# A message-passing layer on one NeuronCore: column addresses kept in DRAM, one resident copy of x, 72 and 68 gathered columns per step, register loads of eight

## The chip, the core and the metric

The kernel runs on one NeuronCore of a Trainium2 chip. The metric is the device time of one execution in microseconds (us). The kernel before takes 5184.74 us, the median of three runs (5167.56 to 5185.11). The profile is of a further execution, of 5200.1 us.

Five engines work side by side: TensorE (PE in the profile, PEld for its weight loads), VectorE (DVE), ScalarE (ACT), GpSimd (POOL) and SyncE (SP), which here only starts DMAs.

## The reference

There are 12500 nodes with 64 features, and 400000 edges sorted by their destination. Each edge has a source `src`, a destination `dst` and 16 features of its own.

```python
src, dst = (edge_index[0], edge_index[1])
m_in = jnp.concatenate([x[src], x[dst], edge_attr], axis=-1)
h = jax.nn.silu(m_in @ W1 + b1)
messages = jax.nn.silu(h @ W2 + b2)
agg = jax.ops.segment_sum(messages, dst, num_segments=x.shape[0])
node_in = jnp.concatenate([x, agg], axis=-1)
return jax.nn.silu(node_in @ W3 + b3)
```

The result is the layer normalisation of x plus what this returns. All of it is float32. The one irregular access is `x[src]`: 400000 rows of 64 numbers at random places.

## The kernel before, in words

**Steps.** The edges are cut into 3125 tiles of 128 edges, and eight tiles make an "oct". There are 391 octs. The main loop, `for o in range(NO + 1)`, issues one oct's work per turn, in a software pipeline. The order of instructions on TensorE, ScalarE, VectorE and SyncE is the order written in the loop. GpSimd's gathers run as far ahead as five buffers (`gat`) allow.

**Three ways to fetch x[src].** The product with the first part of W1 is made once for all nodes and kept in DRAM (`pa`, made by `table` during the first octs). From oct 12 (`RAW`) on:

- *Gathers.* GpSimd starts one indirect DMA for each tile (L373), which fetches 128 rows of `pa` into the buffer `ga`. TensorE later adds them to the oct's first product with an identity matrix (L454), which also frees the buffer.
- *Columns.* x is also held transposed in SBUF (`xs`). For some pairs of tiles, VectorE and ScalarE copy the columns of the 256 edges one by one into a tile `cx`: an instruction copies 64 partitions by 4 bytes, from an address that stands in a register. VectorE does it with a reduction over one element (L297), ScalarE with a copy (L299). TensorE multiplies `cx` by W1 (L451), and GpSimd leaves out these two tiles.
- *Rows.* SyncE starts 16 DMAs of one row per oct (L324); this makes one more pair of tiles in every 16 octs.

**How the columns are dealt.** In each oct VectorE makes 32 columns ahead of the copy `xw` (L402) and the comparison `eh` (L430), and 32 after them. ScalarE makes 32 ahead of the activation `h` (L458) and 28 ahead of the activation `m` (L473). That is 124 in an oct, so a pair of tiles is ready about every 2.06 octs. Ahead of the columns stands a load of registers on the same engine (L290), which reads edge addresses from SBUF. The first load of a run of columns takes 16 registers, the others 8:

```python
ACOLS = (32, 28)
VCOLS = (32, 32)
LOADS = (16, 8)
n = min(hi - lo, P - e0 % P, LOADS[lo > hi - todo])
```

**Where the addresses come from.** For each pair of tiles SyncE loads the 256 sources from DRAM (`index`), and two octs before their use VectorE turns them into byte addresses with two instructions (`address`, L359). The first tile of a pair has its columns read from partitions 0 to 63 of `xs`, the second from partitions 64 to 127, where a second copy of x stands. The second copy is loaded in octs 5 to 8 (`resident(1, c)`).

**VectorE's other work in an oct**: `agg` (L487, adds an oct's sums), `oh` (L424, a comparison ahead of the first columns), `xw` and `eh`. TensorE's first product of the next oct (L441) needs `oh` and `xw`.

Of the kernel before, what the change touches and what calls it, by code (L numbers as in the profile page):

```python
# [11 lines left out]
I32 = mybir.dt.int32  # L12
U8 = mybir.dt.uint8
AF = mybir.ActivationFunctionType
OP = mybir.AluOpType
# [5 lines left out]
P = 128  # L21
# [6 lines left out]
AHEAD = 3  # L28
RAW = 12
TABLES = 7  # L30
ACOLS = (32, 28)
VCOLS = (32, 32)
ROWS = 16
LOADS = (16, 8)
XBASE = (0, 64 << 18)
XADDR = 36864
LAG = CT * P // 32

U = 125
# [4 lines left out]
@with_exitstack  # L44
def kernel(
    ctx: ExitStack,
    tc: tile.TileContext,
    x: bass.AP,
    xt: bass.AP,
    src_c: bass.AP,  # L50
    src_row: bass.AP,
    dst_c: bass.AP,
    dst_row: bass.AP,
    attr_t: bass.AP,
    dst_2: bass.AP,
    attr_2: bass.AP,
    base: bass.AP,
    w1: bass.AP,
    b1: bass.AP,
    w2: bass.AP,  # L60
    b2: bass.AP,
    w3: bass.AP,
    b3: bass.AP,
    out: bass.AP,
    edges: int,
):

    nc = tc.nc
    N, D = x.shape  # L80

    const = ctx.enter_context(tc.tile_pool(name="const", bufs=1))
    dram = ctx.enter_context(tc.tile_pool(name="dram", bufs=1, space=DRAM))
    pa = dram.tile([N, D], F32, name="pa")
    badi = const.tile([1, 1], I32, name="badi")
    ident = const.tile([P, P], F32, name="ident")
    make_identity(nc, ident)

    with ExitStack() as inner:
        windows(inner, tc, ident, badi, pa, x, xt, src_c, src_row, dst_c, dst_row, attr_t, dst_2, attr_2, base, w1, b1, w2, b2, w3, b3, out, edges)  # L90

    flag = nc.values_load(badi[0:1, 0:1], min_val=0, max_val=2 * P,
                          skip_runtime_bounds_check_because="a count of partitions")
    with tc.If(flag > 0):
        general(tc, ident, x, xt, src_c, dst_c, dst_row, attr_t, w1, b1, w2, b2, w3, b3, out, edges)


def windows(ctx, tc, ident, badi, pa, x, xt, src_c, src_row, dst_c, dst_row, attr_t, dst_2, attr_2, base, w1, b1, w2, b2, w3, b3, out, edges):
    nc = tc.nc
    N, D = x.shape  # L100
    NP = xt.shape[1]
    A = attr_t.shape[0]
    TILES = edges // P
# [32 lines left out]
    for s in range(2):  # L136
        h = slice(s * D, (s + 1) * D)
        nc.scalar.dma_start(w1d[h, h], w1[0:D, :])
        nc.scalar.dma_start(b1s[h, :], b1.rearrange("(k o) -> k o", o=1))
    XC = 2048  # L140
    xs = fast.tile([P, NP], F32, name="xs")

    def resident(s, c):
        w = min(XC, NP - c)
        nc.scalar.dma_start(xs[s * D:(s + 1) * D, c:c + w], xt[:, c:c + w])

    resident(0, 0)
    for s in range(2):
        h = slice(s * D, (s + 1) * D)
        nc.scalar.dma_start(w2d[h, h], w2)  # L150
    resident(0, XC)
    w3x = const.tile([D, D], F32, name="w3x")
    b3r = const.tile([1, G, D], F32, name="b3r")

# [1 line left out]
    for s in range(3):  # L156
        part = const.tile([1, D], BF16, name=f"part{s}")
# [32 lines left out]


    agg = fast.tile([P, NP], F32, name="agg")

    bf = fast.tile([1, NO], F32, name="bf")
    nc.vector.tensor_copy(bf, bi)
# [40 lines left out]
    for k in range(3):  # L236
        t = fast.tile([P, P], F32, name=f"xw{k}")
# [10 lines left out]
    with tc.tile_pool(name="gat", bufs=AHEAD + 2) as gat, tc.tile_pool(name="drp", bufs=2) as drp, \  # L248
# [14 lines left out]
        while True:  # L263
            o = RAW + -(-2 * P * (len(pairs) + 1) // RATE) + 1
# [3 lines left out]
        cols, indices = {}, {}  # L268
        xb = xs.bitcast(U8)

        def columns(o, eng, part):
            if o < RAW:
                return
            lo = (o - RAW) * RATE
            if eng == ENG.Activation:
                lo, n = lo + sum(ACOLS[:part]), ACOLS[part]
            else:
                lo, n = lo + sum(ACOLS) + sum(VCOLS[:part]), VCOLS[part]
            hi, todo = lo + n, n
            while lo < hi:  # L280
                j, e0 = lo // (2 * P), lo % (2 * P)
                if j >= len(pairs):
                    return
                n = min(hi - lo, P - e0 % P, LOADS[lo > hi - todo])
                if pairs[j] not in cols:
                    cols[pairs[j]] = cx.tile([P, P], F32, name="cx")
                t = cols[pairs[j]].bitcast(U8)
                s = e0 // P
                h = slice(s * D, (s + 1) * D)
                _, regs = nc.values_load_multi_w_load_instructions(  # L290
                    indices[j][0:1, e0:e0 + n], engines=(eng,), min_val=XBASE[s] + XADDR,
                    max_val=XBASE[s] + XADDR + 4 * (N - 1), skip_runtime_bounds_check_because="src names a node")
                for e, r in zip(range(e0 % P, e0 % P + n), regs):
                    to, frm = t[h, 4 * e:4 * e + 4], xb[h, ds(r - (XBASE[s] + XADDR), 4)]
                    if eng == ENG.DVE:

                        nc.vector.tensor_reduce(to, frm[:, :, None], AX.X, OP.max)  # L297
                    else:
                        nc.scalar.copy(to, frm)  # L299
                lo += n  # L300


        rpairs = []
# [38 lines left out]
        def begun(o):  # L342

            first, behind = -(-(o - RAW) * RATE // (2 * P)), -(-(o + 1 - RAW) * RATE // (2 * P))
            return range(max(0, first), max(0, min(behind, len(pairs))))

        def index(o):
            for j in begun(o):
                t = cxi.tile([1, 2 * P], I32, name="cxi")
                e = octs[pairs[j]][1] * P  # L350
                nc.sync.dma_start(t, src_row[:, e:e + 2 * P])
                indices[j] = t

        def address(o):
            for j in begun(o):
                t = indices[j]
                for s in range(2):
                    h = slice(s * P, (s + 1) * P)
                    nc.vector.tensor_scalar(t[:, h], t[:, h], 4.0, float(XBASE[s] + XADDR), op0=OP.mult, op1=OP.add)  # L359

        winrow, winreg = {}, {}
        sums = psa.tile([P, 4, S], F32, name="pg")
# [71 lines left out]
        def first_layer(o):  # L434
            c, t0, n, first, last = octs[o]
            n2 = n + n % 2
            k = n2 // 2
            ga = got.pop(o)
            oh, eh = hots.pop(o)
            p1 = ps1.tile([P, OT // 2, P], F32, name="p1")  # L440
            nc.tensor.matmul(p1[:, :k], xw[o % 3], oh, start=True, stop=False, skip_group_check=True)  # L441
            if o < RAW:
                pt = mis.tile([P, OT // 2, P], F32, name="mm")
                for i in range(k):
                    nc.tensor.matmul(pt[:, i, :], ga[:, 2 * i:2 * i + 2, :].rearrange("p s d -> p (s d)"), ident,  # L445
                                     start=True, stop=True)
                xg = work.tile([P, OT // 2, P], F32, name="m")
                nc.vector.tensor_copy(xg[:, :k], pt[:, :k])
                nc.tensor.matmul(p1[:, :k], w1d, xg[:, :k], start=False, stop=True, skip_group_check=True)
            if o in pairs:  # L450
                nc.tensor.matmul(p1[:, 0, :], w1d, cols.pop(o), start=False, stop=False, skip_group_check=True)  # L451
            for i in range(1 if o in pairs else 0, k if o >= RAW else 0):
                g2 = single.pop(o) if o in rpairs and i == 1 else ga[:, 2 * i:2 * i + 2, :]
                nc.tensor.matmul(p1[:, i, :], g2.rearrange("p s d -> p (s d)"), ident,  # L454
                                 start=False, stop=(i == k - 1), skip_group_check=True)
            columns(o, ENG.Activation, 0)
            h = work.tile([P, OT // 2, P], F32, name="h")
            nc.scalar.activation(h[:, :k], p1[:, :k], AF.Silu, bias=b1s)  # L458
            made[o] = h, eh
# [138 lines left out]
        with tc.manual_schedule(engines={ENG.PE, ENG.Activation, ENG.DVE, ENG.SP}):  # L598
            compare_dst(0)
            compare_nodes(0)  # L600
            for o in range(NO + 1):
                if o == 0:
                    sources(0, slice(CT, SCT))
                    nc.sync.dma_start(dc[:, CT:SCT], dst_c[:, CT:SCT])
                for k in parts[3 * o - 3:3 * o] if o else []:
                    n = min(XC, NP - k)
                    nc.scalar.activation(agg[:, k:k + n], zero.to_broadcast([P, n]), AF.Copy)
                if o < 2:
                    for c in parts[2:5] if o == 0 else parts[5:]:
                        resident(0, c)  # L610
                if o == 3:
                    for s in range(2):
                        nc.scalar.dma_start(w3s[s * D:(s + 1) * D, :], w3[D:2 * D, :])
# [4 lines left out]
                if o == RAW:  # L618
                    nc.vector.memset(mv, 1.0)
                    nc.vector.memset(eps, 1e-5)  # L620
                if 5 <= o < 5 + (len(parts) + 1) // 2:
                    for c in parts[(o - 5) * 2:(o - 4) * 2]:
                        resident(1, c)
                index(o + 3)
                rload(o + 3)
                if o % (SCT // OT) == 6 and (o // (SCT // OT) + 1) * SCT < TILES:
# [15 lines left out]
                columns(o, ENG.DVE, 0)  # L642
                if o < NO:
                    first_layer(o)
                if o == 0:
                    nc.vector.tensor_copy(b2r, b2p[:, None, :].to_broadcast([3, OT, D]))
                if o + 1 < NO:
# [16 lines left out]
                    add_up(o - 2)  # L664
                if o >= 1:
                    second_layer(o - 1)
                address(o + 2)
                raddress(o + 2)
                rows(o)
                if o < NO:  # L670
# [294 lines left out]
```

## Time and profile before

| What | Value |
|---|---|
| median of three runs | 5184.74 us |
| profiled execution | 5200.1 us, span 5197.9 us |
| TensorE busy (matmul) | 2932.5 us, 56% |
| ScalarE busy | 2906.1 us, 56% |
| VectorE busy | 2641.3 us, 51% |
| GpSimd busy | 2565.3 us, 49% |
| mean granted TensorE clock | 0.629 |
| columns by VectorE (L297) | 24032, 150 ns each |
| columns by ScalarE (L299) | 22560, 188 ns each |
| gathers by GpSimd (L373) | 2619 from `pa`, 944 ns each |

"Busy" counts the time in which an engine executes an instruction. Loads of registers and the starting of DMAs are not counted as busy: they stand in the trace as work of the engine's queue (DVEq, ACTq). An idle time that ended without a semaphore that the profile sees is put down to "issue". The durations of neighbouring columns overlap, so their number times their mean is more than the busy time.

### The profile page before, as it was taken

How to read it: one execution, taken by the hardware profiler on the slowest of the kernel's cores; microseconds unless marked ns; L12 is line 12 of the kernel's file. 1: busy time of each engine (PE TensorE's matmuls, PEld its weight loads, DVE VectorE, ACT ScalarE, POOL GpSimd, SP SyncE). 2: the span in 40 equal slices, each digit the busy share in tenths (PEclk: the TensorE clock that was granted, in tenths of full speed). 3: DMA queues.
4: the chain of work that ended last, by engine and by line, in shares of the span. 5: the costliest groups of instructions: out<-in, count | busy, mean ns of one | idle time of the engine just before them, and what ended most of it. 6: DMA issues, size and time to landing. Idle time of an engine off the chain costs nothing. (4 is left out here: it accounts for less than half of the span.)

```text
span 5197.9 us, 107486 instructions
## 1 busy us (share of the span) xinstructions
PE 2932.5 (56%) x15131; PEld 2075.4 (40%) x15131; DVE 2641.3 (51%) x26395; ACT 2906.1 (56%) x23402; POOL 2565.3 (49%) x2724
## 2 busy tenths in 40 slices
PE   5655655555555555555564655656555555555566
PEld 3443434434433344343343434434433343344344
DVE  1255555545555555555555555555555555555555
ACT  1255555555555655655556565555556555655555
POOL 5544454454444544445444444545454444555453
PEclk7666565666666666666656566565656666665656
DMA  4321111211211121122112211211211221121121
GB/s 85 86 46 39 40 39 40 47 39 40 46 42 43 40 46 40 40 43 42 41 40 49 43 40 42 44 39 40 47 40 40 44 47 40 40 47 39 40 46 40
DMA packets 203943, 229.98 MB, mean 44 GB/s; under 512 B 133612, under 2 KB 141988, under 8 KB 202324
## 3 DMA queue, kind: packets, MB, share of 16 engines
q1 hardware_dynamic: 101528, 122.61, 10.5%
q0 software_dynamic: 86880, 89.14, 9.1%
q10 hardware_dynamic: 14812, 11.26, 0.9%
q14 instruction: 595, 4.87, 0.3%
q8 instruction: 128, 2.10, 0.2%
HBM read 216.36 MB, written 6.40 MB: 43 GB/s over the span
## 5 line engine op out<-in xcount | busy, mean ns | idle before, releaser
L373 POOL DMA_INDIRECT ga<-pa,sc x2619 | 2472.2, 944 | 2516.1 <-PE p L454 1699.8
L299 ACT COPY cx<-xs 64x4 uint8 x22560 | 2404.2, 188 | 1406.1 <-issue 1362.4
L297 DVE TENSOR_REDUCE cx<-xs 64x4 uint8 x24032 | 1910.3, 150 | 1806.6 <-issue 1740.9
L441 PE MATMUL p<-oh,xw 128*128 128x512 f32 (+1 forms) x782 | 772.4, 1089 | 1529.3 <-DVE xw L402 727.6
L441 PEld LDWEIGHTS p<-oh,xw 128*128 128x128 f32 x782 | 187.1, 297 | 1637.1 <-DVE xw L402 776.3
L482 PE MATMUL pg<-eh,m 128*64 128x48 f32 x6250 | 363.0, 277 | 588.6 <-ACT m L473 174.1
L454 PEld LDWEIGHTS p<-ident,ga 128*128 128x128 f32 x2620 | 591.3, 314 | 194.9 <-issue 193.6
L469 PE MATMUL p<-w2d,h 128*128 128x128 f32 x3126 | 642.0, 369 | 1.5 <-issue 1.4
L469 PEld LDWEIGHTS p<-w2d,h 128*128 128x128 f32 x3126 | 545.3, 263 | 133.0 <-issue 133.0
L454 PE MATMUL p<-ident,ga 128*128 128x128 f32 x2620 | 593.2, 397 | 0.0
L482 PEld LDWEIGHTS pg<-eh,m 128*64 128x64 f32 x6250 | 312.1, 189 | 680.2 <-issue 342.2
L473 ACT ACTIVATE m<-p 128x512 f32<-128x512 f32 x391 | 231.8, 593 | 474.9 <-remote 308.9
L458 ACT ACTIVATE h<-p,b1s 128x512 f32<-128x512 f32 x391 | 267.4, 684 | 319.0 <-remote 138.6
L402 DVE TENSOR_TENSOR xw<-mm,mask 96x128 f32<-96x128 f32 x391 | 110.4, 282 | 439.9 <-issue 392.4
L397 PE MATMUL mm<-w1bb,xr 64*96 64x128 f32 x782 | 241.0, 401 | 72.6 <-ACT z L523 49.9
L424 DVE TENSOR_TENSOR oh<-dr,wrow 96x512 f32<-96x512 int32 x391 | 263.6, 674 | 6.3 <-issue 3.5
L430 DVE TENSOR_TENSOR eh<-wrow,dc 128x384 f32<-128x384 f32 x391 | 213.2, 545 | 42.2 <-issue 42.2
L467 PE MATMUL p<-b2r,one 3*128 3x512 bf16 x391 | 194.5, 498 | 0.0
L451 PEld LDWEIGHTS p<-cx,w1d 128*128 128x128 f32 x364 | 116.0, 319 | 175.4 <-issue 175.4
L397 PEld LDWEIGHTS mm<-w1bb,xr 64*96 64x96 f32 x782 | 127.8, 214 | 144.7 <-issue 68.7
L487 DVE TENSOR_TENSOR agg<-agg,pg 128x48 f32 x391 | 77.3, 198 | 123.4 <-remote 32.3
L373 POOL DMA_INDIRECT ga<-in_x,sc x96 | 91.0, 948 | 63.5 <-PE mm L445 28.9
(81 smaller groups left out, 802.7 us busy)
## 6 DMA issues: line engine op xcount, KB each, us to landing
rx<-pa SPq DMA_DIRECT2D x5888, 0.2 KB
dr<-in_dst SPq DMA_DIRECT2D x260, 288.0 KB
ga<-pa,sc POOLq DMA_INDIRECT x2619
oh<-in_attr SPq DMA_DIRECT2D x130, 192.0 KB
xr<-in_xt SPq DMA_DIRECT2D x391, 24.0 KB
xs<-in_xt ACTq DMA_DIRECT2D x12, 512.0 KB
pa<-v ACTq DMA_DIRECT2D x12, 256.0 KB
xa<-in_x SPq DMA_DIRECT2D x24, 128.0 KB
```

The costliest lines, as they stand in the source:

```text
L297: nc.vector.tensor_reduce(to, frm[:, :, None], AX.X, OP.max)
L299: nc.scalar.copy(to, frm)
L373: nc.gpsimd.indirect_dma_start(out=ga[:, i, :], out_offset=None, in_=x if o < RAW else pa[:, :], in_offset=bass.IndirectOffsetOnAxis(ap=sc ...
L397: nc.tensor.matmul(pw[:E, :], winrow[o].rearrange("k s w -> k (s w)"), w1bb.rearrange("k s m -> k (s m)"), start=True, stop=True)
L424: nc.vector.tensor_tensor(oh[:E, :], dr[:, e:e + w], wn[:E, o:o + 1].to_broadcast([E, w]), op=OP.is_equal)
L430: nc.vector.tensor_tensor(eh[:, :n], row[:, None, :].to_broadcast([P, n, S]), rel[:, t0:t0 + n, None].to_broadcast([P, n, S]), op=OP.is_equal)
L441: nc.tensor.matmul(p1[:, :k], xw[o % 3], oh, start=True, stop=False, skip_group_check=True)
L454: nc.tensor.matmul(p1[:, i, :], g2.rearrange("p s d -> p (s d)"), ident, start=False, stop=(i == k - 1), skip_group_check=True)
L458: nc.scalar.activation(h[:, :k], p1[:, :k], AF.Silu, bias=b1s)
L469: nc.tensor.matmul(p2[:, 2 * i:2 * i + 2, :].rearrange("p s d -> p (s d)"), h[:, i, :], w2d, start=False, stop=(i == k - 1), skip_group_ch ...
L473: nc.scalar.activation(m[:, :n2], p2[:, :n2], AF.Silu)
L482: nc.tensor.matmul(pg[s * D:(s + 1) * D, :], m[:, i, :], eh[:, i, :], start=(i < 2), stop=(i >= n - 2), skip_group_check=True)
```

## The change

The column addresses of all edges are made at the start: SyncE loads all of `src` into the space of `agg` as 128 by 3125 numbers, VectorE turns them into addresses with one instruction, and SyncE stores them to a DRAM tensor `adr`. `index` then loads addresses, and `address` is gone with its two instructions for each pair. ScalarE's clearing of `agg` goes through the parts in the reverse order.

There is one copy of x in SBUF, on partitions 0 to 63, and both tiles of a pair read from it; the second tile's columns are still written to partitions 64 to 127. The loads of the second copy in octs 5 to 8 are gone.

VectorE makes 40 and 32 columns in an oct, ScalarE 36 and 32: 140 in all. Every load of registers takes at most eight. Where the program before has 2391 loads and 24032 columns on VectorE, 2352 and 22560 on ScalarE and 2715 gathers, the changed one has 3478 and 26980, 3422 and 25500, and 2669.

```diff
-ACOLS = (32, 28)
-VCOLS = (32, 32)
+ACOLS = (36, 32)
+VCOLS = (40, 32)
 ROWS = 16
-LOADS = (16, 8)
-XBASE = (0, 64 << 18)
+LOADS = 8
 XADDR = 36864
...
-    def resident(s, c):
+    def resident(c):
         w = min(XC, NP - c)
-        nc.scalar.dma_start(xs[s * D:(s + 1) * D, c:c + w], xt[:, c:c + w])
+        nc.scalar.dma_start(xs[:D, c:c + w], xt[:, c:c + w])
...
+    adr = dram.tile([1, TILES * P], I32, name="adr")
+    at = agg[:, :TILES].bitcast(I32)
+
+    def addresses_made():
+        nc.vector.tensor_scalar(at, at, 4.0, float(XADDR), op0=OP.mult, op1=OP.add)
+        nc.sync.dma_start(adr.rearrange("o (p j) -> (o p) j", p=P), at)
...
-                n = min(hi - lo, P - e0 % P, LOADS[lo > hi - todo])
+                n = min(hi - lo, P - e0 % P, LOADS)
...
-                    to, frm = t[h, 4 * e:4 * e + 4], xb[h, ds(r - (XBASE[s] + XADDR), 4)]
+                    to, frm = t[h, 4 * e:4 * e + 4], xb[:D, ds(r - XADDR, 4)]
...
-                nc.sync.dma_start(t, src_row[:, e:e + 2 * P])
+                nc.sync.dma_start(t, adr[:, e:e + 2 * P])
...
-        def address(o):
-            for j in begun(o):
-                t = indices[j]
-                for s in range(2):
-                    h = slice(s * P, (s + 1) * P)
-                    nc.vector.tensor_scalar(t[:, h], t[:, h], 4.0, float(XBASE[s] + XADDR), op0=OP.mult, op1=OP.add)
...
+                if o == 0:
+                    nc.sync.dma_start(at, src_row[:, :TILES * P].rearrange("o (p j) -> (o p) j", p=P))
-                for k in parts[3 * o - 3:3 * o] if o else []:
+                for k in parts[::-1][3 * o - 3:3 * o] if o else []:
...
-                if 5 <= o < 5 + (len(parts) + 1) // 2:
-                    for c in parts[(o - 5) * 2:(o - 4) * 2]:
-                        resident(1, c)
...
+                if o == 1:
+                    addresses_made()
...
-                address(o + 2)
                 raddress(o + 2)
```

More of the change, by code (lines that the diff above doesn't have):

```diff
@@ L89 @@
     with ExitStack() as inner:
-        windows(inner, tc, ident, badi, pa, x, xt, src_c, src_row, dst_c, dst_row, attr_t, dst_2, attr_2, base, w1, b1, w2, b2, w3, b3, out, edges)
+        windows(inner, tc, ident, badi, pa, dram, x, xt, src_c, src_row, dst_c, dst_row, attr_t, dst_2, attr_2, base, w1, b1, w2, b2, w3, b3, out, edges)
     flag = nc.values_load(badi[0:1, 0:1], min_val=0, max_val=2 * P,
@@ L95, with windows @@
         general(tc, ident, x, xt, src_c, dst_c, dst_row, attr_t, w1, b1, w2, b2, w3, b3, out, edges)
-def windows(ctx, tc, ident, badi, pa, x, xt, src_c, src_row, dst_c, dst_row, attr_t, dst_2, attr_2, base, w1, b1, w2, b2, w3, b3, out, edges):
+def windows(ctx, tc, ident, badi, pa, dram, x, xt, src_c, src_row, dst_c, dst_row, attr_t, dst_2, attr_2, base, w1, b1, w2, b2, w3, b3, out, edges):
     nc = tc.nc
@@ L141, in windows @@
     xs = fast.tile([P, NP], F32, name="xs")
-    def resident(s, c):
+    def resident(c):
         w = min(XC, NP - c)
-        nc.scalar.dma_start(xs[s * D:(s + 1) * D, c:c + w], xt[:, c:c + w])
-    resident(0, 0)
+        nc.scalar.dma_start(xs[:D, c:c + w], xt[:, c:c + w])
+    resident(0)
     for s in range(2):
@@ L150, in windows @@
         nc.scalar.dma_start(w2d[h, h], w2)
-    resident(0, XC)
+    resident(XC)
     w3x = const.tile([D, D], F32, name="w3x")
@@ L269, in windows, with pieces @@
         xb = xs.bitcast(U8)
-        def columns(o, eng, part):
+        def pieces(o, eng, part):
             if o < RAW:
@@ L278, in columns @@
                 lo, n = lo + sum(ACOLS) + sum(VCOLS[:part]), VCOLS[part]
-            hi, todo = lo + n, n
+            hi = lo + n
             while lo < hi:
@@ L283, in columns, with addresses @@
                     return
-                n = min(hi - lo, P - e0 % P, LOADS[lo > hi - todo])
+                n = min(hi - lo, P - e0 % P, LOADS)
+                yield j, e0, n
+                lo += n
+        def addresses(eng, j, e0, n):
+            _, regs = nc.values_load_multi_w_load_instructions(
+                indices[j][0:1, e0:e0 + n], engines=(eng,), min_val=XADDR,
+                max_val=XADDR + 4 * (N - 1), skip_runtime_bounds_check_because="src names a node")
+            return regs
+        def columns(o, eng, part):
+            for j, e0, n in pieces(o, eng, part):
+                regs = addresses(eng, j, e0, n)
                 if pairs[j] not in cols:
@@ L289, in columns @@
                 h = slice(s * D, (s + 1) * D)
-                _, regs = nc.values_load_multi_w_load_instructions(
-                    indices[j][0:1, e0:e0 + n], engines=(eng,), min_val=XBASE[s] + XADDR,
-                    max_val=XBASE[s] + XADDR + 4 * (N - 1), skip_runtime_bounds_check_because="src names a node")
                 for e, r in zip(range(e0 % P, e0 % P + n), regs):
-                    to, frm = t[h, 4 * e:4 * e + 4], xb[h, ds(r - (XBASE[s] + XADDR), 4)]
+                    to, frm = t[h, 4 * e:4 * e + 4], xb[:D, ds(r - XADDR, 4)]
                     if eng == ENG.DVE:
@@ L299, in columns @@
                         nc.scalar.copy(to, frm)
-                lo += n
         rpairs = []
@@ L609, in windows @@
                     for c in parts[2:5] if o == 0 else parts[5:]:
-                        resident(0, c)
+                        resident(c)
                 if o == 3:
```

## The prediction

> **What bounds the kernel now.** I first read the list of who waited for whom, because busy shares near 50% on every engine say nothing.
>
> ```profile
> DVE cx L297 <- issue: 1740.9, 2985, 5.5
> POOL ga L373 <- PE p L454: 1699.8, 322, 12.3
> ACT cx L299 <- issue: 1362.4, 2046, 5.6
> PEld p L441 <- DVE xw L402: 776.3, 161, 9.7
> ```
>
> GpSimd waits 1700 us for TensorE to free gather buffers, so it isn't the bound. TensorE waits for VectorE's `xw`. VectorE's largest wait is "issue", on its columns: nobody holds it up, its own queue does. From other engines it waits only some 170 us (L487, 123 us; L402, 47 us). So VectorE's instruction stream sets the pace.
>
> Second, that stream in a quiet oct, by the timeline of VectorE:
>
> ```profile
> 3621.69 0.54 DVE L430 TENSOR_TENSOR eh<-wrow,dc 128x384 f32<-128x384 f32 x1
> 3622.32 1.78 DVE L297 TENSOR_REDUCE cx<-xs 64x4 uint8 x24
> 3624.41 0.62 DVE L297 TENSOR_REDUCE cx<-xs 64x4 uint8 x8 [0.30 <-issue]
> 3625.25 0.21 DVE L487 TENSOR_TENSOR agg<-agg,pg 128x48 f32 x1 [0.23 <-PE p L454]
> 3625.37 0.68 DVE L424 TENSOR_TENSOR oh<-dr,wrow 96x512 f32<-96x512 int32 x1
> 3626.58 1.75 DVE L297 TENSOR_REDUCE cx<-xs 64x4 uint8 x24 [0.53 <-issue]
> ```
>
> Columns follow each other at 64 ns, but there is a hole ahead of a group. The line of the register loads tells why:
>
> ```profile
> L290 DVEq TENSOR_LOAD <-cxi x6: 593/598/1100, 3621.1 to 3628.0; - x6
> ```
>
> (minimum, median, maximum in ns.) Over the whole trace a load of 4 takes 0.34 us, of 8 0.60, of 12 0.85, of 16 1.10: about 63 ns a register. Undisturbed, the next load begins 0.917 us after a load of 8 with its columns, and 1.661 us after one of 16 (lowest twentieth of each). The columns alone would take 0.51 and 1.02. So VectorE's queue, not its arithmetic, is full.
>
> Third, the same engines while GpSimd gathers, and after it stops, by a table of stretches (an "x" is a count):
>
> ```profile
> core 0: us, PE busy (x) PEld busy (x) DVE busy (x) ACT busy (x) POOL busy (x), PEclk, DMA share, GB/s
> ...
> 3603.00:3610.50 7.50, 4.05 (x12) 2.46 (x10) 1.81 (x11) 1.78 (x12) 4.72 (x5) 0.50 0.16 31
> ...
> 3637.40:3643.00 5.60, 5.50 (x33) 3.96 (x34) 4.80 (x57) 5.56 (x47) 1.14 (x2) 0.62 0.36 86
> ```
>
> In the first stretch VectorE and ScalarE get 11 and 12 instructions done in 7.5 us, one or two per 0.71 us and in step with each other; in the second, 57 and 47 in 5.6 us. These stalls begin some 3 us after a burst of gathers begins. Counting gaps of 0.5 to 1.5 us common to VectorE, ScalarE and SyncE, a burst of six gathers (178 of them) brings 4.5 us of stall, one of eight (177) brings 7.3. Start to next start is 12.48 us after six and 14.08 after eight. About half the time is stall; 22% of the columns get done in it. An oct (median 13.1 us) is then a stall whose length GpSimd's burst sets, plus a quiet part that VectorE's queue fills.
>
> **The change part by part.**
>
> *More columns and smaller loads on VectorE.* From 0.917 and 1.661, a column costs the queue (1.661 - 0.917)/8 = 93 ns and a load 0.917 - 8 x 0.093 = 173 ns. There are 26980 - 24032 = 2948 more columns, 274 us, and 3478 - 2391 = 1087 more loads, 188 us: **+462 us** if all of it falls into quiet parts. If 22% is done within stalls as now, it is 0.78 x 462 = **+360 us**. I take 360: the 170 us of waits for others can also give way. Per oct: two runs of 16+8+8 cost 6.99 us, nine loads of eight 8.25.
>
> A rule speaks on this price. The Trainium skill, "DMA: Bandwidth & Descriptors", section "Latency and other measured facts", gives tensor_load a floor of about 600 ns, with unrolling to spread it. Read as a price by the load, 1087 more would cost 652 us, and halving a load of 16 would save nothing. The rows show 0.60 for eight but 0.34 for four, growing with the registers, so the rows decide: 462.
>
> *The first load of eight, not 16*, ends 0.5 us earlier and removes the hole of 0.53 after `oh`. The queue is full, so this only moves the hole to the added load; it is in the sum above. It is what the rival below lives on.
>
> *ScalarE.* 2940 more columns at 95 ns start to start are 279 us. Its loads are hidden: columns behind a later load of eight start 95 ns after the one before (median). In a quiet oct ScalarE needs 60 x 0.095 + 0.68 + 0.59 = 6.97 us, then 7.74; VectorE's queue needs over 8.25. ScalarE waits 319 us ahead of `h` and 475 ahead of `m` now. Nothing added; if VectorE's load were hidden, this would be the next bound, at most +279.
>
> *Addresses.* 364 instructions (L359) go. In quiet octs the way from the second run's load to the next oct's first load is 4.36 us with them and 4.09 without: 182 x 0.27 = **-49 us**. What is late next is the same load, behind `oh`.
>
> *Gathers.* 46 fewer. By the starts of bursts one is worth (14.08 - 12.48)/2 = 0.8 us, by the stalls 1.4: 37 to 64, I take **-50 us**. The skill's "SBUF — State Buffer", section "Who interferes with whom", says that ScalarE never waits on anyone and that only VectorE shares a port with GpSimd; by it a gather less on an idle GpSimd is worth 0. The table of stretches shows ScalarE stalled with VectorE, so I keep 50.
>
> *Start.* Oct 12 begins at 206.5 us. 3.2 MB of loads of the second copy go (ScalarE's queue, after 131 us; a few us at most). Added on SyncE are a load and a store of 1.6 MB, ahead of window loads (L392) that waited there up to 38 us for TensorE anyway. At the 85 GB/s of the page's first slice each takes an estimated 19 us: the load, started at about 21 us, is there by 40. VectorE's one address instruction stands behind `m` (L448, done 69 us) and ahead of `xw`: 3125 elements at `oh`'s 512 in 0.67 us are 4 us, hidden behind TensorE's tables (71 to 78 us), 4 us if not. The store then ends at about 92 us. ScalarE's clearing of the reused part waits for it; it stood at 85 to 90 us, and behind it are queued `h` of oct 2 and the tables: some 4 us late. Bounds -15 to +20, taken 0.
>
> *Reading partitions 0 to 63, writing 64 to 127*: no row shows it. The nearest is the same instruction on one set, 64 ns. I take no difference; 10 ns on half of VectorE's columns, were the queue not ahead, would be +135 us; a gain has no source.
>
> Sum: 360 - 49 - 50 + 0 = +261. On the profiled 5200 that is 5461; the median lies 15 lower, so about **5450 us**.
>
> **The rivals.**
>
> *Faster: the loads hide.* If the queue runs ahead far enough that all loads but the first are covered, as on ScalarE, shorter first loads pay: the holes ahead of both runs (0.39 and 0.24 us by the loads' times) go, 0.63 x 377 = -238 us. Columns cost 2948 x 64 ns = +189, addresses and gathers -99: -148, about 5040. It decides where eight columns (0.51 us) cover a load of eight (0.60 plus 0.09 to the first column); the holes of 0.30 ahead of eights speak against. **13%.**
>
> *No change: stalls set the pace.* If the added work fits into stalls or waits for others, only -99 plus up to a quarter of 462 stays: 5170 to 5210. Against it: 22% of the columns in half the time. **7%.**
>
> *Forecast*, 5250 to 5600: the top is 462 - 49 - 37 = +376 with up to 40 from the start or the partitions, the low end half of 360 less 99. **73%.**
>
> *Slower still: stalls lengthen with the instructions.* If a stall serves a number of instructions, not a time, 12% more columns lengthen half the span by 12%: +310 on top, about 5750. The stalls' lengths of 4.5 and 7.3 by gathers speak against. **7%.**
>
> **How the numbers follow.** The measurement tells about 0.5% from no change. Slower 73 + 7 = 80%, same 7%, faster 13%. Range 5160 to 5600: it takes in no change, and leaves out the rival ends.
>
> **What would show it.** L297's load-to-load time of eights stays 0.917 and its "issue" wait grows by some 250 us; bursts of six stay at 4.5 us of stall. TensorE's wait for `xw` grows. Wrong if the holes ahead of eights vanish (then faster), if ScalarE has no wait left ahead of `m`, or if columns written across partitions are over 64 ns apart.

## The result, and the profile after

The changed kernel takes 5501.55 us (median of four runs, 5498.24 to 5504.95) against 5184.92: a ratio of 1.0616 (95% interval 1.0589 to 1.0643). It is slower by 317 us, where 265 were forecast. The profiled execution took 5504.7 us, its span 5502.9.

The list of who waited for whom, of the changed kernel (us in total, times, longest), shows the same engines waiting for each other as before:

```profile
POOL ga L382 <- PE p L463: 2129.7, 359, 11.0
PEld p L450 <- DVE xw L411: 2061.7, 304, 10.0
DVE cx L314 <- issue: 1966.2, 3794, 4.8
PE p L450 <- DVE xw L411: 1941.5, 296, 9.8
ACT cx L316 <- issue: 1236.1, 1815, 5.5
ACT m L482 <- remote: 650.3, 216, 9.0
DVE xw L411 <- issue: 271.8, 135, 7.0
PEld p L450 <- remote: 184.8, 27, 9.3
PEld pg L491 <- ACT m L482: 75.0, 26, 8.4
```

Two lines of the kernel before belong beside these:

```profile
PEld p L441 <- remote: 712.7, 122, 9.7
DVE xw L402 <- issue: 392.4, 151, 6.3
```

VectorE's "issue" time ahead of columns grew from 1741 to 1966 us, that is by 225, near the 250 named in the prediction. About half of this growth is a shift, since the same wait ahead of `xw` fell from 392 to 272; most of what VectorE's time grew by besides is busy time (2641 to 2818 us). TensorE's wait for `xw` grew from 776 to 2062 us. Part of this is a shift too: for the same product the wait that the profile puts down to nobody it knows ("remote") fell from 713 to 185. Together they grew from 1489 to 2247, by 758: VectorE is later than before, and TensorE waits for it. GpSimd waits 2130 us for buffers and is further from being the bound.

A quiet stretch of VectorE, from its timeline, shows where its time goes now:

```profile
3019.11 0.54 DVE L439 TENSOR_TENSOR eh<-wrow,dc 128x384 f32<-128x384 f32 x1
3019.58 0.58 DVE L314 TENSOR_REDUCE cx<-xs 64x4 uint8 x8
3020.34 0.59 DVE L314 TENSOR_REDUCE cx<-xs 64x4 uint8 x8 [0.18 <-issue]
3021.26 0.60 DVE L314 TENSOR_REDUCE cx<-xs 64x4 uint8 x8 [0.33 <-issue]
3022.18 0.59 DVE L314 TENSOR_REDUCE cx<-xs 64x4 uint8 x8 [0.32 <-issue]
3022.70 0.19 DVE L496 TENSOR_TENSOR agg<-agg,pg 128x48 f32 x1
3022.80 0.67 DVE L433 TENSOR_TENSOR oh<-dr,wrow 96x512 f32<-96x512 int32 x1
3023.53 0.60 DVE L314 TENSOR_REDUCE cx<-xs 64x4 uint8 x8
3024.45 0.60 DVE L314 TENSOR_REDUCE cx<-xs 64x4 uint8 x8 [0.32 <-issue]
```

The hole of 0.53 us after `oh` is gone, as a shorter first load should have it. In its place stands a hole of 0.3 us ahead of nearly every further eight columns, and the eights start 0.92 us apart: 3020.34, 3021.26, 3022.18. Before, 24 columns went by in 1.78 us with one such hole behind them. The line of the register loads in this stretch (3019.1 to 3027.8) gives their durations, minimum, median and maximum in ns:

```profile
L297 DVEq TENSOR_LOAD <-cxi x10: 592/597/709, 3018.7 to 3027.5; - x10
```

And the table of stretches, the first of them quiet, the second in a burst of gathers:

```profile
core 0: us, PE busy (x) PEld busy (x) DVE busy (x) ACT busy (x) POOL busy (x), PEclk, DMA share, GB/s
...
3019.10:3027.80 8.70, 6.43 (x37) 4.52 (x37) 6.52 (x76) 8.10 (x70) 3.33 (x4) 0.70 0.13 30
3028.00:3033.30 5.30, 0.00 (x0) 0.00 (x0) 0.00 (x0) 0.00 (x0) 4.03 (x5) 0.50 0.15 28
```

In the second, five gathers start while TensorE, VectorE and ScalarE execute nothing for 5.3 us. The stalls are as long as before. To compare the two profiles I count as stall each time of 0.5 to 1.5 us in which none of VectorE, ScalarE and SyncE starts an instruction (a little narrower than the prediction's count). A burst of six gathers then brings 4.0 us before and 4.1 after, a burst of eight 6.7 and 6.7; in all 2021 us before and 1970 after. The count is good to some 60 us: the first kernel below, with the gathers of the kernel before, has 1963. So the loss lies outside the stalls, where the time of the two profiles grew from 3177 to 3533 us. Oct 12 begins at 205.0 us instead of 206.5, so the start of the kernel neither gained nor lost.

### The profile page after: what moved, and what is told of

Same layout as the page of the kernel before. It is cut to its first block, busy times and chain, and to the rows that moved or that the text cites. A ratio compares the mean times of both kernels' runs of the same rounds, so it can differ in the third digit from the quotient of the medians.

```text
span 5502.9 us, 114510 instructions
## 1 busy us (share of the span) xinstructions
PE 2881.6 (52%) x15131; PEld 2036.9 (37%) x15131; DVE 2817.6 (51%) x28980; ACT 3234.7 (59%) x26342; POOL 2529.5 (46%) x2678
## 5 line engine op out<-in xcount | busy, mean ns | idle before, releaser
L382 POOL DMA_INDIRECT ga<-pa,sc x2573 | 2435.1, 946 | 2855.1 <-PE p L463 2129.7
L316 ACT COPY cx<-xs 64x4 uint8 x25500 | 2736.0, 189 | 1268.9 <-issue 1236.1
L314 DVE TENSOR_REDUCE cx<-xs 64x4 uint8 x26980 | 2156.4, 141 | 2034.8 <-issue 1966.2
L450 PE MATMUL p<-oh,xw 128*128 128x512 f32 (+1 forms) x782 | 794.0, 1118 | 2213.9 <-DVE xw L411 1941.5
L478 PE MATMUL p<-w2d,h 128*128 128x128 f32 x3126 | 584.9, 344 | 1.8 <-issue 1.8
L478 PEld LDWEIGHTS p<-w2d,h 128*128 128x128 f32 x3126 | 494.6, 241 | 121.1 <-issue 121.1
L406 PE MATMUL mm<-w1bb,xr 64*96 64x128 f32 x782 | 224.5, 376 | 59.2 <-ACT z L532 37.6
L460 PEld LDWEIGHTS p<-cx,w1d 128*128 128x128 f32 x410 | 135.7, 331 | 207.9 <-issue 207.9
L476 PE MATMUL p<-b2r,one 3*128 3x512 bf16 x391 | 181.8, 465 | 0.0
L460 PE MATMUL p<-cx,w1d 128*128 128x128 f32 x410 | 128.1, 415 | 0.0
```

Source lines behind the costliest of these rows:

```text
L382: nc.gpsimd.indirect_dma_start(out=ga[:, i, :], out_offset=None, in_=x if o < RAW else pa[:, :], in_offset=bass.IndirectOffsetOnAxis(ap=sc ...
L406: nc.tensor.matmul(pw[:E, :], winrow[o].rearrange("k s w -> k (s w)"), w1bb.rearrange("k s m -> k (s m)"), start=True, stop=True)
L478: nc.tensor.matmul(p2[:, 2 * i:2 * i + 2, :].rearrange("p s d -> p (s d)"), h[:, i, :], w2d, start=False, stop=(i == k - 1), skip_group_ch ...
```

## The experiments

The theory is that of the prediction: VectorE's queue, with a price for each column and each load, fills the quiet parts of an oct, and GpSimd's bursts set the length of the stalls. The rivals are that the addresses or the write across partitions cost the time, that the holes decide and not the number of loads, that ScalarE shares the price, and that the stalls come from the loads themselves.

The runs were made in three groups of four, each group on one chip together with the kernel before; differences in us between groups are therefore between chips, and the ratios say how far they hold. On the chips of the first and the third group the kernel before took 5189 and 5184 us. On the chip of the second it took 3432, which was not expected, and which the last section takes up. Ratios are always to the kernel before on the same chip.

**The old column counts.** The changed kernel with

```diff
-ACOLS = (36, 32)
-VCOLS = (40, 32)
+ACOLS = (32, 28)
+VCOLS = (32, 32)
```

> The changed kernel with the old column counts (32 and 32 on VectorE, 32 and 28 on ScalarE); addresses once, one copy of x and loads of eight stay. VectorE's queue as the bound: eight loads of eight in an oct cost 8 x 0.917 = 7.34 us against 6.99 before, +0.35 x 376 = +130 us, nine tenths of it (what the change itself showed of its 462) is +117, less 49 for the addresses: about 5250 us. If smaller first loads pay because the hole ahead of the columns goes: 5185 - 238 - 49, about 4900. If the price of the change lies in the addresses or in writing across partitions and not in the columns: still near 5500.

Measured: 5195 us, a ratio of 1.0017 (1.0000 to 1.0034). Addresses, one copy of x, columns written across partitions and loads of eight together cost next to nothing. The loss lies in the number of columns. It was 55 us less than the queue's price said, so the loads of eight are cheaper than I made them, or the addresses saved more; this run doesn't separate the two, and the next one speaks for the loads. This kernel has 2619 gathers, as the one before.

**The old loads.** The changed kernel with its 72 and 68 columns, and

```diff
-LOADS = 8
+LOADS = (16, 8)
...
-                n = min(hi - lo, P - e0 % P, LOADS)
+                n = min(hi - lo, P - e0 % P, LOADS[lo > hi - todo])
```

> The changed kernel with the old loads: the first of a run takes 16 registers, the others 8; 72 and 68 columns stay. VectorE's queue: an oct costs 1.661 + 3 x 0.917 + 1.661 + 2 x 0.917 = 7.91 us against 8.25, -0.34 x 375 x 0.9 = -115: about 5385 us. If the loads of eight are what keeps the loss small (holes ahead of the first column come back, 0.63 us an oct): about 5740. If the number of loads has no price at all: 5500.

Measured: 5454 us, 1.0510 (1.0483 to 1.0536), 47 us below the changed kernel (44 to 55 by the ratios). The direction is the queue's: fewer, longer loads are faster, though the hole ahead of the first column comes back. The size is four tenths of its price of 115: 703 fewer loads on VectorE (2775 against 3478) at about 67 ns each. The rival, holes as the deciding thing (5740), is out.

**Columns added on VectorE alone**, with `ACOLS = (32, 28)` in the changed kernel.

> The changed kernel with ScalarE back at 32 and 28 columns, VectorE at 40 and 32 (132 in an oct). VectorE's queue: VectorE's work is that of the changed kernel, and there are about 22 gathers more at 1 us: 5520 us. If ScalarE's 8 columns carried part of the loss: down to 5350.

Measured: 5538 us, 1.0668 (1.0642 to 1.0695). Against the first run, which differs only in VectorE's eight columns and one load an oct, this is +343 us. Eight columns and a load at the queue's price, 0.917 us in 376 octs, are 345. But this kernel also has 22 gathers fewer than the first run's; at the prediction's 1.1 us each the columns and loads then cost some 367, so at least the whole price. The changed kernel, which has ScalarE's eight columns on top, is 37 us *faster* (27 to 38 by the ratios), and it has 24 gathers fewer: at 1.4 us of stall a gather that is 34. Two lines of this run's waits, which the next run is read against:

```profile
PEld p L450 <- DVE xw L411: 2065.7, 301, 9.9
ACT m L482 <- remote: 1684.0, 316, 9.0
```

VectorE's eight were added ahead of `xw`, for which TensorE waits. Whether they would cost as much behind it (32 and 40) was not run, so the price of their place is not told apart from that of the queue.

**Columns added on ScalarE alone**, with `VCOLS = (32, 32)` in the changed kernel.

> The changed kernel with VectorE back at 32 and 32 columns, ScalarE at 36 and 32 (132 in an oct). VectorE's queue: VectorE's work is that of the first of these four kernels, and there are about 22 gathers fewer: 5230 us. If ScalarE's 8 columns (0.76 us an oct) are on the path too: up to 5500.

Measured: 5301 us, 1.0203 (1.0175 to 1.0230). This is 106 us over the first run, where I had expected some 20 less: with 64 columns on VectorE, ScalarE's eight do count. The list of waits of this run shows a wait that the changed kernel hardly has (75 us there) and that the first run has at 273, while the wait for `xw` is nearly gone:

```profile
PEld pg L491 <- ACT m L482: 1151.5, 198, 17.5
PE pg L491 <- ACT m L482: 1084.8, 183, 17.3
PEld p L450 <- DVE xw L411: 47.3, 16, 6.9
```

TensorE waits for ScalarE's second activation, behind its columns. So the two engines were close to each other before the change. With 72 columns on VectorE, ScalarE waits instead (`m`, 1684 us in the run above, 650 in the changed kernel), and its own columns are free. So the engines' prices depend on each other: VectorE's eight cost 343 us with 60 columns on ScalarE, and 201 (this run to the changed kernel) with 68.

**No gathers, and four gathers** (second group, on the chip where the kernel before takes 3432 us; `KEPT` is 0 and 4). In the changed kernel, from oct 12 on, tiles beyond the first `KEPT` of an oct are not gathered but taken as zeros from a fixed tile:

```diff
+KEPT = 0
...
-            for i in range(n):
+            for i in range(n if o < RAW else min(n, KEPT)):
...
-                g2 = single.pop(o) if o in rpairs and i == 1 else ga[:, 2 * i:2 * i + 2, :]
+                g2 = single.pop(o) if o in rpairs and i == 1 else (ga if 2 * i < KEPT else gz)[:, 2 * i:2 * i + 2, :]
```

> The changed kernel without the gathers of the table from oct 12 on: the eight tiles of an oct (but for those made by columns and rows) add zeros from a fixed tile, so their part of x[src] is left out of the result. If GpSimd's gathers cause the stalls: VectorE and ScalarE never step at 0.7 us, and an oct takes VectorE's quiet time, 8.25 us of columns and some 0.6 of other queue work: 8.9 x 379 + 205 = about 3570 us. If the stalls come from the loads of registers or from the columns' own addresses: they stay, and the time is over 5000.

> The changed kernel with gathers for the first four tiles of an oct alone (two to four of them after columns and rows); the other four add zeros, so their part of x[src] is left out. Bursts of four gathers stood by 1.6 to 1.8 us of stall, so if a stall begins only some 3 us into a burst, nearly all stall goes: (8.9 + 0.7) x 379 + 205 = about 3850 us. If each gather costs the same 1.4 us of stall: 2.2 gathers leave 3 us, about 4700.

Measured: 3689 us without gathers (1.0747, 1.0725 to 1.0768) and 3688 with four (1.0745, 1.0723 to 1.0766). On this chip neither says what it was made for, since stalls are missing with four gathers as without. What they do show is the kernel with hardly any gathers, where VectorE's queue was to be the bound: GpSimd is busy 3% or 30% of the span, and the time is the same, 3% over the 3570 expected. Even without gathers this is slower than the whole kernel before on that chip.

**Columns on ScalarE alone, and no columns** (second group), `VCOLS = (0, 0)` in the changed kernel, and `ACOLS = (0, 0)` as well.

> The changed kernel without columns on VectorE, 36 and 32 on ScalarE (68 in an oct). About 7.5 gathers an oct, 9.4 us of GpSimd and by bursts of six and eight some 6.5 us of stall. VectorE's queue as the bound: it goes, and ScalarE's 7.74 us of quiet time (less what it does within stalls, a fifth) sets the oct: 6.5 + 6.2 = 12.7 us, about 5000. If ScalarE would hold the oct up as much as VectorE did: 5400 and over.

> The changed kernel without any columns; GpSimd gathers all tiles but for SyncE's rows. If columns on VectorE and ScalarE, made between stalls, cost more than the gathers they spare: GpSimd becomes the bound with 7.9 gathers at 1.25 us, 9.9 us an oct, stalls and the other engines' work beside it: about 4100 us, at most 4600. If gathers are the scarce thing and stalls then fill the time: over 5200.

Measured: 3658 us (1.0655, 1.0638 to 1.0673) and 3886 (1.1318, 1.1299 to 1.1337). The expectation for the first was made for a chip with stalls and is not tested by it; the second came in below the 4100 expected, with no stalls beside the gathers. In both GpSimd gathers almost without a pause, 1.249 us from one to the next: without stalls, gathers are the scarce thing, and columns pay, up to the 124 an oct of the kernel before.

**The changed kernel again** (third group).

> The changed kernel as it stands, beside the kernel before on the same chip. Where the kernel before takes about 5185 us: 5500 again. Where it takes about 3430 (no stalls): VectorE's queue is the bound even so, since the changed kernel without any gathers took 3689 there; so about 3690, a ratio of 1.075. If the loss needs the stalls: no slower than the kernel before.

Measured: 5502 us, 1.0594 (1.0569 to 1.0619): the result again, on the chip of the third group. Whether the change also loses where there are no stalls was not run; the run without gathers (1.0747) points that way.

**One load ahead of each run of columns** (third group): the first run's kernel with

```diff
-LOADS = 8
+LOADS = 32
```

> Old column counts (32 and 32, 32 and 28), addresses once, one copy of x, and one load of up to 32 registers ahead of each run of columns. By the queue's prices (93 ns a column, 173 a load) an oct costs VectorE 2 x 3.15 = 6.30 us against 7.34 with loads of eight and 6.99 before. Where the kernel before takes 5185: between 4805 (all of 1.04 x 376 off the 5195 of loads of eight) and 5040 (four tenths, as the change from 16 to 8 showed). If what counts is the hole ahead of the first column, a load of 2.1 us stands bare twice an oct: about 5700. Where the kernel before takes 3430 and GpSimd is the bound: 3400 to 3430.

Measured: 5095 us, 0.9814 (0.9794 to 0.9833), faster than both kernels, by 1.9% than the one before, and short of the 4805 to 5040 expected. Per load saved the gain is again smaller than the price: 100 us below loads of eight, a quarter of 1.04 x 376 = 391. VectorE's loads here (minimum, median, maximum in ns), and the next wait in the list:

```profile
L297 DVEq TENSOR_LOAD <-cxi x912: 341/2099/2382, 213.3 to 5043.3; - x183
```

```profile
PEld pg L491 <- ACT m L482: 658.6, 176, 12.5
PE pg L491 <- ACT m L482: 609.5, 163, 12.3
```

A load of 32 takes 2.10 us, on the line of 63 ns a register. Once VectorE is quicker TensorE waits for ScalarE (273 us with loads of eight), as with 64 and 68 columns above: part of the gain may have gone there, but no run tests it.

**No gathers, on a chip with stalls** (third group), the kernel of the second group.

> The changed kernel without gathers of the table from oct 12 on (that part of x[src] left out), again. Where the kernel before takes 5185 (chip with stalls): if it needs gathers to bring the stalls on, 3690 as on the chip without stalls; if instructions alone stall, over 5000. Where the kernel before takes 3430: 3690.

Measured: 3728 us, 0.7186 (0.7172 to 0.7200). Without gathers the stalls are gone on this chip too, and the time is within 1.1% of that on the other. So the loads and the columns don't bring the stalls on; the gathers do. Two lines of this run, the wait of VectorE ahead of its columns and the register moves with which SyncE starts its row DMAs (ns, minimum, median, maximum):

```profile
DVE cx L315 <- issue: 742.5, 2277, 0.7
L341 SPq MOVE rx<-pa x5888: 29/29/40, 184.1 to 3611.3; - x197
```

The longest such wait is 0.7 us, where the changed kernel has 4.8, and of its 1966 us some 740 remain. The larger part of VectorE's "issue" is thus the stalls, and not the work of its own queue. The timeline of VectorE shows an undisturbed oct, from one `xw` to the next:

```profile
2600.46 0.29 DVE L418 TENSOR_TENSOR xw<-mm,mask 96x128 f32<-96x128 f32 x1
2600.66 0.54 DVE L446 TENSOR_TENSOR eh<-wrow,dc 128x384 f32<-128x384 f32 x1
2601.22 1.30 DVE L315 TENSOR_REDUCE cx<-xs 64x4 uint8 x16
2602.85 0.60 DVE L315 TENSOR_REDUCE cx<-xs 64x4 uint8 x8 [0.33 <-issue]
2603.77 0.60 DVE L315 TENSOR_REDUCE cx<-xs 64x4 uint8 x8 [0.32 <-issue]
...
2609.23 0.27 DVE L418 TENSOR_TENSOR xw<-mm,mask 96x128 f32<-96x128 f32 x1
```

That is 8.77 us, against 8.25 for nine loads of eight and their columns.

**No columns, on a chip with stalls** (third group).

> The changed kernel without any columns, again. Where the kernel before takes 5185: GpSimd gathers without a pause, so stalls never end; the some ten steps of VectorE and ScalarE in an oct at 0.7 us still fit into GpSimd's 9.9 us: about 4000 us, faster than both kernels. If stalls under unbroken gathering grow with the gathers (1.4 us for each of 7.9): 5000 and over. Where the kernel before takes 3430: 3886 as before.

Measured: 5206 us, 1.0038 (1.0016 to 1.0061). I had expected 4000, so this theory of mine fell: I had counted the stalled steps of VectorE and ScalarE, and forgotten SyncE's. The list of waits of this kernel (of an execution with a span of 5253 us) begins:

```profile
DVE oh L435 <- DMA dr<-in_dst: 1732.0, 105, 28.9
PEld mm L408 <- DMA xr<-in_xt: 1449.9, 167, 19.0
```

VectorE and TensorE wait for loads that SyncE starts. SyncE starts 16 row DMAs an oct ahead of them, each with a register move. One oct's 16 (start, duration in us), here:

```profile
2607.51 14.83 SPq L340 DMA_DIRECT2D rx<-pa  x16
```

and of the same kernel on the chip without stalls:

```profile
2607.67 5.09 SPq L340 DMA_DIRECT2D rx<-pa  x16
```

The lines of these moves, again here and there (ns, minimum, median, maximum):

```profile
L340 SPq MOVE rx<-pa x5888: 2/29/1397, 208.9 to 5153.9; - x197
```

```profile
L340 SPq MOVE rx<-pa x5888: 29/29/42, 140.9 to 3748.1; - x197
```

The median is 29 ns on both, but a move takes up to 1397 ns under gathers on one chip and never over 42 on the other. SyncE's own list of steps is then what is late. That it is the row DMAs that make it late was not tried alone.

## Why the prediction was right

The direction and the mechanism are right. The size, 5450 forecast and 5502 measured, is in part luck: two of its terms were wrong by 40 and 100 us, in opposite directions.

*VectorE's queue sets the quiet part.* Right: 0.917 us from load to load held (median 0.92 in the changed kernel), TensorE's wait for `xw` grew, and VectorE's columns alone reproduce the loss (third run against the first, +343), though by their number or by their place ahead of `xw` is not told apart. Columns written across partitions were 64 ns apart (median), as before. The reading that "nobody holds it up, its own queue does" goes too far: most of VectorE's "issue" goes away with the gathers.

*The term that was mis-sized* is the factor 0.78 in "0.78 x 462 = +360 us". I had let 22% of the added work fall into stalls. Counted on both profiles as above, only about a tenth of VectorE's columns start within stalls: 8% before and 9% after where steps less than 0.25 us apart are joined, 11 and 10% between the first and the last step of each burst. In the third run VectorE's added columns with their load were paid at least in full: 343 us beside 22 gathers spared, where the price is 345.

*The loads' share was too high*, and this hid the error above. 173 ns for each of 1087 loads are 188 us; going from 16 to eight measured 47 us where the price says 115, and from eight to 32 a quarter of it. Some of a load's time is covered. With the load at the 67 ns of the second run, the first run's 705 added loads cost 47 us and the addresses save 49, an estimate of -2 where +10 was measured; so the cheaper load explains that run. A column is then dearer than 93 ns: an estimate of 118 from the third run (367 us less 378 loads at 67 ns, over 2896 columns). The queue price is the sum of two parts, and only the whole, eight columns with their load, was tested at full size. What covers the rest isn't settled: with loads of 32 TensorE waits for ScalarE next, and with loads of 16 it waits more for ScalarE's `m` (245 us) than in the changed kernel (75), but no run takes ScalarE out of the way.

Put in order, from the kernel before: old counts with all the rest +10, VectorE's columns +343, ScalarE's with the gathers that they spare -37. Their sum is the measured loss by construction, and the parts depend on the order: with ScalarE's columns first the steps are +10, +106 and +201. The forecast had, for the first order, about +50, +240 and -25. The first was too high and the second too low, and the errors all but cancel.

*Gathers.* "I take -50" for 46, about 1.1 us each; the last step gives 37 us for 24 gathers (27 to 38 by the ratios), at ScalarE's cost of nothing 1.1 to 1.6 each. That leans to the bound by the stalls, 1.4 against 0.8, without settling it. The Trainium skill's rule that ScalarE never waits on anyone, in "SBUF — State Buffer", section "Who interferes with whom", speaks of SBUF's ports. The stalls found here reach SyncE's register moves as well (up to 1397 ns instead of 29). The rule says nothing of these, and no run shows where the stalls lie.

*ScalarE.* "Nothing added" holds at 72 columns on VectorE and fails at 64 (+106). My account left out that VectorE's queue and ScalarE stood so near each other: 8.25 us against 7.74 was its own sum.

*Start, addresses, partitions.* All taken at or near nothing, and together they are (+10 with the loads of eight).

*The rivals.* Hidden loads are out: the holes ahead of eights stayed at 0.32. Stalls that lengthen with instructions are out: 4.1 and 6.7 us a burst, as before. For "no change" the terms named, -99 and up to a quarter of 462, make 5086 to 5200, not the 5170 to 5210 that stand there.

## What to carry to other kernels

When an engine waits for "issue", first take out the stalls that it shares with other engines (here the larger part), then price its queue, not its arithmetic: take the time from one register load to the next, with all that stands between. Work that is moved from one engine to another to spare a third pays only as long as the receiver isn't the one that sets the pace; here 128 columns on two engines spared one gather of 1.25 us and cost VectorE's queue alone some 7.5 us (its 66 of them, in eights at 0.917). Where a stall has a fixed length, don't count on it to take up added work.

## What the runs showed of the hardware that was not expected

The same kernel takes 5184 to 5189 us on two chips and 3432 on a third. Where it is slow, VectorE, ScalarE and SyncE step together at about 0.7 us while GpSimd's gathers run, from some 3 us into a burst; on the third no trace shows it, with gathers at the same 1.249 us (the register moves above). Those traces are of the four kernels of the second group; of the kernel before there are only times there. Taking the gathers out ends the stalls on a chip that has them (5502 to 3728). What the chips differ in, or whether it is the chip at all and not its state in that hour, is not shown by any run. For this kernel it turns the trade around: without columns the time is 13% longer where there are no stalls, and 0.4% longer where there are.

Register loads cost by the register: 0.34, 0.60, 0.85, 1.10 and 2.10 us for 4, 8, 12, 16 and 32 on VectorE.
